# The first attention of a two-layer attention kernel: folding work dealt last, the last pair's inverses and division sooner, and the planned order from four units ahead of the projection

## The chip, the cores and the metric

The kernel runs on one core of a Trainium2 chip. The metric is the device time of one execution in microseconds (us); a measurement is the median of several runs. The core has a matrix engine (TensorE, called PE in the profile), three engines for elementwise work (VectorE or DVE, ScalarE or ACT, GpSimd or POOL), and SyncE (SP), which here only issues DMAs. Each engine works through its own list of instructions in order and waits for the others at semaphores. [...]

## The reference

Two layers work on x (8, 512, 32, 32), batch by batch; T = 1024 positions, 512 channels. Cut to what matters:

```python
# layer 0: eight heads of 64 channels
h = group_norm(xf)
qkv = einsum('oc,bct->bot', qkv_w, h) + qkv_b
q, k, v = (fake_quant(t) for t in split(qkv))     # 8 bits; minimum and maximum over the whole tensor
w = softmax(einsum('bct,bcs->bts', q * scale, k * scale))
a = einsum('bts,bcs->bct', w, v)
x = xf + einsum('oc,bct->bot', proj_w, a) + proj_b
# layer 1: one head of 512 channels
t = tokens(group_norm(x))
q, k, v = t @ wq.T + bq, t @ wk.T + bk, t @ wv.T + bv
out = softmax(q @ k.T / sqrt(512)) @ v
x = x + tokens_back(out @ wp.T + bp)
```

## The kernel before, in words

A first phase (up to about 581 us) norms x, forms q, k and v of all batches, stores them to HBM and collects their extremes, since the quantization needs these over the whole tensor. Then comes a second phase, which the change concerns: attention of layer 0, the projection and layer 1, batch by batch.

**Units.** Layer 0's attention is a generator, `attention()`. Two heads make a pair; a batch has four pairs, written (batch, pair). A unit is one step u: for a pair and one half (512) of the queries, one block s of 128 keys. A pair has 16 units, a batch 64, so units 0 to 63 are batch 0 and unit 64 begins pair (1,0). For each unit TensorE forms the scores `st` (`scores`, line 1007), ScalarE takes their exponential into a tile `pt`, `spare` or `aside`, and the result is split (`split`, line 1038) into an f16 part and the rest in f16, both in `two`: one engine casts, and VectorE subtracts the cast from the exponential (`rest`). In batch 0 the cast is a DMA issued by GpSimd for s = 0, 1 and 4, VectorE's for s = 6, and ScalarE's for s = 2 and 5; blocks s = 3 and 7 stay f32 (`aside`) and are not split. From batch 1, s = 2 and 6 are cast by GpSimd. TensorE then forms the weighted sums of v (`av`) and the sums of the exponentials (`sm`). `scores` runs six to nine units ahead of the weighted sums: a turn of the generator, four units long, begins with the scores of units u+6 and u+7 and ends with the split of u+8 and u+9.

**Work of a pair.** `load_pair` (line 937) fetches q, k and v of the next pair and puts their quantizing on VectorE: two instructions each for q, k and v, and a third for v in batch 0. `finish` (line 1128), after a pair's second half, copies the sums, gathers them into `apart` by two small DMAs, and leaves two pieces of work: `spread`, which adds and inverts them, writes them to HBM and fetches them back broadcast over the partitions; and `divide`, which divides the pair's output `ao`. The projection needs all four.

**Folding.** Layer 1's weights are multiplied with one another ahead of their use (`fold`, line 1734): wq with wk into `wa`, wv with wp into `wm`. The generator yields after each product, 36 steps in all; six of them (`HELD`) are kept for batch 0's layer 1. The others are taken by TensorE, nine ahead of unit 0 and 21 in `scores` (line 1014), one at a time. A fold of two has four products of four steps, then a weighing of the bias and a sum. It also leaves VectorE work: five pieces named "fold", each over `fold_room` or the widened `z`, which the weighing needs, and four named "wa".

**Who orders VectorE.** TensorE's order is that of the text. In the first attention the order of VectorE and ScalarE is that of the text too (`InOrder.strict`); work that is not tied to a unit waits in a list, `dealt`, of entries (unit from which it is due, name, work). At each split, `deal(u)` (line 919) does the first entry of the list that is due, and no more than one; fetching v goes along with the entry ahead of it. `settle(name)` does all of a name at once, where they are needed at the latest: quantized q and k ahead of the first scores of a pair, the divisions ahead of the projection. A cast by DMA is kept in `put_off`, and its subtraction is put in at the split three units later, or where it is needed.

After batch 0's attention and `LEAD` = 2 further turns (units 64 to 71), `InOrder.planned` is set (line 1888): from then on a planner keeps a clock for TensorE, VectorE and ScalarE, adds each operation's cost, and fits side work (`later`, with a time at which it is ready and one at which it is due) into the gaps that it foresees. Then `project(0)` follows, whose half of 16 f32 products is split by one turn of attention, and layer 1 of batch 0 with further turns between.

Of the kernel before, what the change touches and what calls it, by code (L numbers as in the profile page):

```python
# [25 lines left out]
PAIRS = HEADS // 2  # L26
# [20 lines left out]
LEAD = 2  # L47
# [11 lines left out]
def attn_pair_kernel(  # L59
# [97 lines left out]
    def elements(n):  # L157

        return 0.21 + n * 0.957e-3
# [147 lines left out]
    with ExitStack() as fast:  # L307
# [39 lines left out]
        cut, at = {}, 0  # L347
# [44 lines left out]
        with tc.tile_pool(name="p1w", bufs=1) as p1w, tc.tile_pool(  # L392
            name="p1", bufs=2
# [519 lines left out]
        def plain(b, s):  # L913
            return b == 0 and s % 4 == 3
# [2 lines left out]
        dealt = []  # L917

        def deal(u):
            i = next((i for i, (at, *_) in enumerate(dealt) if at <= u), None)  # L920
            if i is not None:
                dealt.pop(i)[2]()
                if dealt[i : i + 1] and dealt[i][2].__name__ == "fetch_v":
                    dealt.pop(i)[2]()
# [12 lines left out]
        def load_pair(b, j, u=None):  # L937

            nm = f"{b}_{j}"
            raws = []  # L940

            def fetch(i, src):
                if (b, j, i) == (0, 0, 2):
                    raw = aop.tile([P, NH, 512], F32, tag="ao", name="raw_first").rearrange(
                        "p h n -> p (h n)"
                    )
                else:
                    raw = raw_p.tile([P, T], F32, tag="raw", name=f"raw_{nm}_{i}")
                nc.sync.dma_start(
                    raw if i < 2 else raw.rearrange("p (t d) -> p t d", t=NT), src  # L950
                )
                raws.append(raw)

            def whole(raw, _, i):
                quant2(raw.rearrange("p (t d) -> p t d", t=NT)[:, 3::4, :], vfs[j], i)

            fetch(0, q_d[b][j])
            fetch(1, k_d[b][j])
            qt = qkp.tile([P, T], BF, tag="q", name=f"q_{nm}")
            kt = qkp.tile([P, T], BF, tag="k", name=f"k_{nm}")  # L960
            vt = qkp.tile([P, NT, P], F16, tag="v", name=f"v_{nm}")
            todo = (qt, kt, vt.rearrange("p t d -> p (t d)"))

            if b == 0:
                vfs[j] = xp.tile([P, 2, 256], F32, tag="x", name=f"vf_{nm}")[:, :, 0:P]

            def quants(i):
                for n, step in enumerate((quant, quant2, *([whole] if i == 2 and b == 0 else []))):
                    name, work = "qk" if i < 2 else "qv", lambda step=step: step(raws[i], todo[i], i)
                    if u is None or InOrder.planned:  # L970
                        dve.later(name, 0.7, work, pe.t + 12.0, 45.0)
                    else:
                        dealt.append((u + (7, 9, 15)[i] + n, name, work))
                        if (i, n) == (0, 1):
                            dealt.append((u + 8, "qk", fetch_v))

            def fetch_v():
                if len(raws) == 2:
                    fetch(2, v_d[b][:, :, bass.ts(j, P)])
                quants(2)  # L980

            if (b, j) == (0, 0):
                fetch(2, v_d[b][:, :, bass.ts(j, P)])
            quants(0)
            quants(1)
            if u is None or InOrder.planned:
                dve.later("qk", 0.0, fetch_v)
            return qt, kt, vt
# [4 lines left out]
        def attention():  # L993
# [13 lines left out]
            def scores(u):  # L1007
                b, j, hf, s = units[u]
                if hf == 0 and s == 0:
                    settle("qk")  # L1010
                nm = f"{b}_{j}_{hf}"
                qt, kt, _ = pairs[b, j]
                st = pair_ps(f"st_{nm}_{s}")
                if (u < 10 or u % 5 == 0) and fold_left[0] > HELD:
                    fold_step()
                awaits(st_free[-2])
                for i, r in enumerate(HALF):
                    mm(
                        st[:, i, :], lhsT=kt[r, bass.ts(s, P)],
                        rhs=qt[r, bass.ts(hf, 512)], start=True, stop=True,  # L1020
                    )
                if u >= 4:
                    need(u - 4)
                if plain(b, s):
                    pt = aside[:, u // 4 % 3].rearrange("p (i k) n -> p i (k n)", i=2)
                elif u < BY_DMA and s in CAST_BY_DMA:
                    at = (u // NT * len(CAST_BY_DMA) + CAST_BY_DMA.index(s)) % 3
                    pt = spare[:, 1 + 2 * at : 3 + 2 * at].rearrange("p i k n -> p i (k n)")
                else:
                    pt = ptp.tile([P, 2, 512], F32, tag="p", name=f"pt_{nm}_{s}")  # L1030
                there = act.do(
                    1.12, lambda: act.activation(pt, st, AF.Exp, scale=esc),
                    max(pe.t + 0.25, ready.get(u - 4, 0.0) + 0.1),
                )
                st_free.append(there)
                pts[u] = pt, there

            def split(u):

                b, j, hf, s = units[u]  # L1040
                pt, there = pts.pop(u)
                if not InOrder.planned:
                    for v in [v for v in put_off if v < u - 2]:
                        put_off.pop(v)()
                    deal(u)
                if plain(b, s):
                    parts[u], ready[u] = pt, there
                    return
                two = partp.tile([P, 2, 2, 512], F16, tag="two", name=f"two_{b}_{j}_{hf}_{s}")
                parts[u] = two  # L1050

                def rest():
                    dve.tensor_tensor(two[:, 1], pt, two[:, 0], ALU.subtract)
                    ready[u] = dve.t

                if u < BY_DMA and s in CAST_BY_DMA:
                    nc.gpsimd.dma_start(two[:, 0], pt)
                    put_off[u] = rest
                    return

                def cast(copy=act.copy):
                    at_hand.add(u)
                    copy(two[:, 0], pt)  # L1063
                    done_at = act.t if copy == act.copy else there + 1.5
                    dve.later("sum", elements(1024), rest, done_at + 0.1, 9.0)

                if b == 0:
                    cast(dve.tensor_copy if s in CAST_BY_DVE else act.copy)
                elif s % 4 == 2:
                    cast(nc.gpsimd.tensor_copy)  # L1070
                elif not InOrder.planned and s == 5:
                    cast(dve.tensor_copy)
                else:
                    act.later("cast", 1.02, cast, there, 7.0)
# [53 lines left out]
            def finish(b, j, hf, u):  # L1128
# [30 lines left out]
                def spread():  # L1159
                    r = rcs[:, n * 16 : (n + 1) * 16]  # L1160
                    dve.tensor_add(r, apart[:, 0, :], apart[:, 1, :])
                    dve.reciprocal(r, r)
                    nc.sync.dma_start(rs_d[n].rearrange("r (p k) -> (r p) k", k=16), r)
                    for i, r in enumerate(HALF):
                        nc.sync.dma_start(
                            rs[r], rs_d[n][2 * i : 2 * i + 2, :].partition_broadcast(CH)
                        )
                    if InOrder.planned:
                        dve.later("ao", elements(1100), divide, dve.t + 7.0, 20.0)
                    else:  # L1170
                        dealt.append((u + 20, "ao", divide))

                if InOrder.planned:
                    dve.later("ao", 0.4, spread, pe.t + 5.0, 8.0)
                else:
                    dealt.append((u + 12, "ao", spread))

            for u in (0, 2, 4):
                for i in (u, u + 1):
# [671 lines left out]
        def advance():  # L1851
            nonlocal done
            done = next(att, B)

        def others():
            steps = None
            for b in range(B):
                if steps is None:
                    yield from project(b)
                    steps = norm1(b)  # L1860
                steps = yield from layer1(b, steps)
# [12 lines left out]
        InOrder.strict = True  # L1874
        while done < 1:
            advance()
        for _ in range(LEAD):
            advance()
        while fold_left[0] > HELD:
            fold_step()  # L1880
# [2 lines left out]
            const.tile([P, 1], F32, name="second_pow"), fourth[:, 0:1], mhalf[:, 0:1], ALU.pow  # L1883
        )
        tc.add_manual_dep(warm.ins, dve.last.name, IN_ORDER, reason="order")
        for e in (dve, act):
            e.t = pe.t
        InOrder.planned = True
        for n in others():
            dense, late = n < 0, n == 2  # L1890
            advance()
# [364 lines left out]
```

## Time and profile before

| | us |
|---|---|
| median of 3 runs (2586.36 to 2592.11) | 2586.4 |
| the profiled execution, its own time | 2591.22 |
| its span in the profile | 2589.4 |
| first scores of unit 0 | 590.68 |
| first scores of units 16, 32, 48, 64 | 617.78, 647.42, 672.24, 696.65 |
| last sums of batch 0's attention end | 705.07 |
| first and second half of the first projection begin | 716.02, 743.15 |

The profile is of one execution, traced by the hardware. Its page gives the busy time of each engine as a share of the span and, in 40 slices of the span (64.7 us each), the busy tenths and the clock that TensorE was granted, in tenths of full speed. A line of the view of waits names the engine and tile that waited, after the arrow the engine and tile it waited for, and then the total in us, the number of times and the longest. A line of the timeline has the start and the length in us, the engine, the line of the kernel (often that of a helper: 91 for VectorE and ScalarE, 209 for TensorE), the operation, the output and inputs with their shapes, the number of instructions merged, and in brackets the idle time just before and what ended it. An f32 product leaves two records on TensorE.

### The profile page before, as it was taken

The numbers are of one execution on the slowest core, as the hardware profiler recorded it, in microseconds if no ns is written. First come the engines' busy times: TensorE is split into PE (matmuls) and PEld (weight loads), VectorE is DVE, ScalarE is ACT, GpSimd is POOL, SyncE is SP. The second block draws the span as 40 slices with busy tenths as digits, with TensorE's granted clock in tenths as the row PEclk, the third lists the DMA queues.
The fourth block names the chain that finished last, engine by engine and source line by source line (L and its number), as shares of the span: only waits on it lengthen the run. The fifth ranks groups of instructions, "written<-read, shape, count | busy, mean of one in ns | idle before, by whom it ended". The sixth has DMA issues, their size and how long they took to land.

```text
span 2589.4 us, 38715 instructions
## 1 busy us (share of the span) xinstructions
PE 2526.8 (98%) x15670; PEld 1751.5 (68%) x15670; DVE 1898.0 (73%) x2748; ACT 1346.6 (52%) x1683; POOL 186.1 (7%) x167
## 2 busy tenths in 40 slices
PE   7999999998989999999999999999999999999998
PEld 4788888872247765775677577657756775777687
DVE  6787777668868777777877788777777777775544
ACT  3222222217947665665566566747665665664121
POOL 0000000001100001000100010010001000100000
PEclk9899999999999999999999999999999999999999
DMA  4333333336622232223222331232232123212211
GB/s 168 129 145 135 117 119 122 130 122 172 152 80 73 67 110 98 62 78 111 86 58 79 116 97 58 95 116 61 78 107 98 46 79 123 83 54 83 86 37 39
DMA packets 160189, 250.69 MB, mean 97 GB/s; under 512 B 27008, under 2 KB 93568, under 8 KB 158464
## 3 DMA queue, kind: packets, MB, share of 16 engines
q1 hardware_dynamic: 125264, 182.81, 21.2%
q10 hardware_dynamic: 30560, 57.71, 6.5%
q0 software_dynamic: 4176, 7.60, 1.7%
q8 instruction: 125, 2.05, 0.3%
q14 instruction: 64, 0.52, 0.1%
HBM read 153.64 MB, written 86.28 MB: 93 GB/s over the span
## 4 chain that ended last, share of the span: by engine, by line
PE 84%; DVE 6%; ACT 3%; issue 1%; DMA 1%; POOL 0%; SPq 0%; ACTq 0%; DVEq 0%; POOLq 0%
PE s L209 15%; PE o L209 13%; PE qkps L209 12%; PE pj L209 9%; PE av L209 7%; PE v2ps L209 7%; PE vps L209 6%; PE g L209 6%; PE st L209 4%; PE sm L209 3%; DVE two L91 2%; ACT pt L91 1%; DVE h L91 1%; PE fold L209 1%; DVE acc L91 1%
## 5 line engine op out<-in xcount | busy, mean ns | idle before, releaser
L91 ACT ACTIVATE pt<-st,esc 128x1024 f32<-128x1024 f32 x467 | 496.6, 1115 | 343.0 <-PE st L209 328.5
L91 DVE TENSOR_TENSOR two<-pt,two 128x1024 f16<-128x1024 f32 x467 | 562.4, 1218 | 145.7 <-POOL two L1063 102.9
L91 ACT CAST two<-pt 128x1024 f16<-128x1024 f32 x345 | 349.9, 1055 | 6.1 <-ACT p L91 5.1
L209 PE MATMUL av<-two,v 128*32 128x512 f16 x3968 | 246.0, 381 | 4.5 <-DVE two L91 3.3
L1063 POOL CAST two<-pt 128x1024 f16<-128x1024 f32 x112 | 146.3, 1306 | 1418.1 <-ACT pt L91 720.4
L209 PE MATMUL s<-g,h 128*128 128x256 f32 x1024 | 233.4, 380 | 0.0
L209 PE MATMUL pj<-ao,wp 128*128 128x512 f32 x512 | 226.3, 600 | 6.2 <-DVE ao L91 6.2
L209 PEld LDWEIGHTS s<-g,h 128*128 128x128 f32 x1024 | 193.0, 190 | 30.9 <-issue 4.3
L91 ACT ACTIVATE u_ring<-qkps,qkbt 128x512 f32<-128x512 f32 x89 | 61.1, 687 | 253.1 <-PE qkps L209 236.2
L209 PEld LDWEIGHTS <-v 128*32 128x32 f16 x3968 | 91.7, 96 | 142.2 <-issue 66.3
L209 PEld LDWEIGHTS pj<-ao,wp 128*128 128x128 f32 x512 | 97.0, 192 | 129.3 <-issue 112.0
L209 PE MATMUL st<-q,k 64*128 64x512 bf16 x1024 | 163.5, 382 | 17.3 <-ACT pt L91 4.9
L209 PE MATMUL s<-g,sums 128*128 128x256 f32 x768 | 178.5, 381 | 0.2 <-DVE p L91 0.2
L209 PE MATMUL o<-p,v 128*128 128x256 f32 x768 | 175.2, 382 | 1.0 <-DVE p L91 1.0
L209 PEld LDWEIGHTS o<-p,v 128*128 128x128 f32 x768 | 144.3, 190 | 27.1 <-issue 5.7
L209 PEld LDWEIGHTS s<-g,sums 128*128 128x128 f32 x768 | 144.6, 190 | 24.5 <-issue 4.6
L209 PE MATMUL sm<-two,ones 128*32 128x512 f16 x1984 | 136.2, 380 | 0.0
L209 PE MATMUL qkps<-half,w_high 128*128 128x512 f32 x480 | 134.5, 403 | 0.0
L209 PE MATMUL qkps<-half,w_low 128*128 128x512 f32 x480 | 132.4, 398 | 1.9 <-DVE half L91 1.9
L209 PEld LDWEIGHTS <-k 64*128 64x128 bf16 x1024 | 34.6, 94 | 146.6 <-issue 139.9
L209 PE MATMUL qkps<-half,w_mix 128*128 128x512 f32 x480 | 132.6, 399 | 0.6 <-DVE half L91 0.6
L209 PE MATMUL v2ps<-wm,h 128*128 128x256 f32 x512 | 119.9, 383 | 1.9 <-ACT g L91 1.3
(225 smaller groups left out, 3909.8 us busy)
## 6 DMA issues: line engine op xcount, KB each, us to landing
rs<-rs_d SPq DMA_DIRECT2D x76, 256.0 KB
x<-in_x_dram SPq DMA_DIRECT2D x32, 512.0 KB
q_d<-wa SPq DMA_DIRECT2D x32, 512.0 KB
k_d<-wa SPq DMA_DIRECT2D x32, 512.0 KB
v_d<-v_ring SPq DMA_DIRECT2D x32, 512.0 KB
raw<-q_d SPq DMA_DIRECT2D x32, 512.0 KB
raw<-k_d SPq DMA_DIRECT2D x32, 512.0 KB
x_d<-h SPq DMA_DIRECT2D x64, 256.0 KB
```

Of the source, the lines that this page charges most:

```text
L91: ins = self.latest = op(*args, **kw).ins
L209: ins = nc.tensor.matmul(ps, lhsT=lhsT, rhs=rhs, **kw).ins
L1063: copy(two[:, 0], pt)
```

## The change

Seven edits, all in the order of work; no product or operation of the computation is added or taken away.

```diff
         def deal(u):
-            i = next((i for i, (at, *_) in enumerate(dealt) if at <= u), None)
-            if i is not None:
+            due = [i for i, (at, *_) in enumerate(dealt) if at <= u]
+            if due:
+                i = next((i for i in due if dealt[i][1] not in ("fold", "wa")), due[0])
                 dealt.pop(i)[2]()
...
-                        dealt.append((u + (7, 9, 15)[i] + n, name, work))
+                        at = u + (7, 9, 15)[i] + n + (8 if b and j else 0)
+                        dealt.append((at, name, work))
                         if (i, n) == (0, 1):
-                            dealt.append((u + 8, "qk", fetch_v))
+                            dealt.append((at, "qk", fetch_v))
...
-                if (u < 10 or u % 5 == 0) and fold_left[0] > HELD:
+                if (u < 4 or u % 4 == 1) and fold_left[0] > HELD:
                     fold_step()
...
                     deal(u)
+                else:
+                    for v in list(put_off):
+                        at_hand.add(v)
+                        dve.later("sum", elements(1024), put_off.pop(v), pe.t, 9.0)
...
-                        dealt.append((u + 20, "ao", divide))
+                        dealt.append((u + (20 if j < PAIRS - 1 else 11), "ao", divide))
...
-                    dealt.append((u + 12, "ao", spread))
+                    dealt.append((u + (12 if j < PAIRS - 1 else 7), "ao", spread))
...
-        for _ in range(LEAD):
+        for _ in range(LEAD - 1):
             advance()
...
-        for e in (dve, act):
-            e.t = pe.t
+        dve.t, act.t = pe.t + 4.5, pe.t + 2.0
         InOrder.planned = True
+        for _, name, work in dealt:
+            dve.later(name, 0.7, work, pe.t + 10.0, 24.0)
+        dealt.clear()
+        advance()
         for n in others():
```

1. `deal` prefers a due entry that is not folding work ("fold" or "wa") and falls back on folding work.
2. The quantizing of a later pair of a later batch, which in the unplanned part is pair (1,1) alone, is due eight units later, and its fetch of v with q's second instruction.
3. The fold steps are taken at units 0 to 3 and then at every fourth unit (5, 9, 13, ... 69) instead of at units 0 to 9 and every fifth (10, 15, ... 60). The weighing of the first fold goes from unit 7 to unit 17.
4. Subtractions still put off when planning begins are given to the planner.
5. For the last pair of a batch in the unplanned part (units 48 to 63), the inverses are due at unit 67 instead of 72 and the division at 71 instead of 80.
6. Planning begins after the turn of unit 64 instead of after that of unit 68. The turn of unit 68 is then planned; the position of the projection in TensorE's order stays.
7. The planner's clocks of VectorE and ScalarE start 4.5 and 2.0 us ahead of TensorE's instead of level with it, and the entries left in `dealt` become side work of the planner.

## The prediction

> **What bounds the kernel now.** I read the page first: who is busy, and in which slices.
>
> ```profile
> PE 2526.8 (98%) x15670; PEld 1751.5 (68%) x15670; DVE 1898.0 (73%) x2748; ACT 1346.6 (52%) x1683; POOL 186.1 (7%) x167
> PE   7999999998989999999999999999999999999998
> PEclk9899999999999999999999999999999999999999
> ```
>
> TensorE is busy 98% of the span, so time can only come from its few waits or from its work, and the change alters no product. Next, the waits of TensorE alone, from 580 to 800 us, where the first attention and the first projection lie.
>
> ```profile
> PE pj L209 <- DVE ao L91: 6.2, 1, 6.2
> PE st L209 <- DVE k L91: 4.6, 1, 4.6
> PE av L209 <- DVE two L91: 3.3, 5, 1.3
> ...
> PE wt_f L209 <- DVE spare L91: 1.4, 1, 1.4
> ...
> PE av L209 <- DVE v L91: 1.1, 1, 1.1
> ```
>
> Two waits stand out, once each: the scores of pair 2 (unit 32) for its keys, and the projection for the last pair's division. From 735 us to the end the same view adds up to 9.8 us, the longest 1.3; so nothing large is to be had later. The timeline of TensorE at the two waits:
>
> ```profile
> 642.17 0.61 PE L209 MATMUL sm<-two,ones 128*32 128x512 f16 x8
> 647.42 0.60 PE L209 MATMUL st<-q,k 64*128 64x512 bf16 x4 [4.64 <-DVE k L91]
> ...
> 648.78 1.93 PE L209 MATMUL av<-aside,vf 128*32 128x512 f32 x8
> ...
> 716.02 2.84 PE L209 MATMUL pj<-ao,wp 128*128 128x512 f32 x6
> 725.06 5.24 PE L209 MATMUL pj<-ao,wp 128*128 128x512 f32 x6 [6.20 <-DVE ao L91]
> ```
>
> After each wait the work is slow for some us: aside's eight products take 1.93 instead of 1.03, six records of the projection 5.24 instead of 2.84. By the starts of the following instructions that costs 1.6 and 2.1 us. VectorE's timeline says what is late:
>
> ```profile
> 627.88 0.69 DVE L91 CUSTOM_DVE_ANT_0 fold_room<-wn_v,gn_row 128x512 f32<-128x512 f32 x1
> ...
> 635.55 0.68 DVE L91 TENSOR_SCALAR spare<-ones,z 128x32 f32<-128x32 f32 x4
> ...
> 646.62 0.75 DVE L91 TENSOR_SCALAR k<-raw,bhi 128x1024 bf16<-128x1024 f32 x1
> ...
> 714.55 1.01 DVE L91 TENSOR_TENSOR rcs<-apart 128x16 f32<-128x16 f32 x1
> ...
> 723.73 1.28 DVE L91 SCALAR_TENSOR_TENSOR ao<-ao,scl,kept_u 128x1024 f32<-128x1024 f32 x1 [1.44 <-DMA kept_u<-rs_d]
> ```
>
> Five pieces of folding work and two loads stood ahead of pair 2's quantizing, so k came at 646.62. The last pair's inverses came at 714.55, though its sums were complete at 705.07 (the end of aside's last sums).
>
> **What the Trainium skill says.** "TensorE: Matmul & The Clock Gate", What's actually happening: an idle window of about 3.4 us halves the clock for about as long. The trace agrees: waits of 4.64 and 6.20 us were followed by slow products, that of 1.43 us (at 600.76) was not. "Trainium Architecture — The Big Picture", Inside one NeuronCore: each engine has its own instruction stream and meets the others only at semaphores; so what stands behind a waiting division waits as well, as here the 7 us of TensorE behind ao. "DMA: Bandwidth & Descriptors", Issuing engines are not separate DMA queues: all DMAs share 16 engines. The trace agrees: the casts by DMA took 6.4 us to land in 600 to 614 us, beside the 2 MB load of x, and 3.4 in 614 to 640.
>
> **The change part by part.** I worked the dealing rule through by hand, unit by unit, for both kernels; the old order reproduces VectorE's timeline.
>
> Folding dealt last. Pair 2's k moves from the deals at units 30 and 31 to 26 and 27, some 6 us sooner (1.5 us a unit). It is 4.6 us late, so that wait goes: 4.6 gained. The slow 1.6 after it I don't count: the pair after the wait took 24.8 us (672.24 less 647.42), the next one 24.4, as ScalarE sets the pace there (24.14 busy of 25 us, 680 to 705). The folding work, four at 0.69 and 0.16 + 0.68, is 3.6 us; it goes to units 36 to 45. There VectorE has, for a pair, 12 subtractions at 1.14, 2 casts at 0.7, 4.4 of quantizing, 1.6 of inverses and division, so 21.1, and with it 24.7 against a pair of 24.4: I charge 0.5.
>
> Fold steps spread out. Units 0 to 15 had 12 steps and get 7; the weighing goes from unit 7 to 17. ScalarE's waits for TensorE there were 0.46, 1.44, 0.26 and 1.88, and a copy of 0.59 moves away: up to 4.4 could go. But the weighted sums of units 4 and 5 need subtractions that VectorE, busy without a gap from 596, ends at 605.2; following ScalarE from there, unit 16 starts at 614.4 instead of 617.78: 3.4 gained. The steps reappear: 12 instead of 9 in units 16 to 61, and two at 65 and 69, each 1.06 to 1.13 us of TensorE. TensorE had 22.79 busy of 25 us (680 to 705), so 2.2 free a pair, and one step more fits; if it didn't, it would cost 1.1 a pair. I charge 0.3 for the three pairs and 1.0 of the 2.2 for the last two, where the gaps were only 0.61 and 0.27.
>
> DMAs and queues. The 2 MB load of x frees with the weighing, so SP issues it near 616 instead of 602.28; it meets the casts by DMA of units 16, 17 and 20, whose subtractions came 5.6 us after issue. With 6.4 of landing that is 0.8 charged. At worst three casts are late by 3: 3 us.
>
> The last pair. The inverses are dealt at unit 68 (was 72), the division at 71 (was 80). Count from T, the end of the last sums (705.07 before). The two gathers are issued at T+1.2; elsewhere an 8 KB gather lands 2.7 after (937.59 to 940.31): T+3.9. VectorE, free at T+2.5, waits 1.4 there, and the inverses end at T+4.3. Write issued T+4.5, broadcast 1.5 later (777.23 to 778.67), landing 4.6 to 6.2 after that (1308.44 to 1313.03; 717.51 to 723.73): T+10.6 to T+12.2. Behind the inverses stand unit 69's cast and subtraction, then 70's and 68's: done near T+8.4 instead of T+7.8. Then VectorE waits for the broadcast, and behind the division (1.2) stands unit 71's subtraction (1.14): T+13.0 to T+14.6. TensorE, which had passed at T+9.5, wants that at about T+10.5: the wait has moved from the projection to the weighted sums, and is 2.5 to 4.1 us. 1.0 us of products later the projection starts, at T+14.0 to T+15.6, and its first half takes 13.75 without a break: T+27.8 to T+29.4, where it ended at T+33.74 (738.81). That is 4.4 to 6.0 gained, less 0 to 2.1 if the clock drops again. I take 4.0; the bounds are 0 (a gather late by 4 us) and 8.3 (6.2 + 2.1, all of it).
>
> Planned order four units sooner. Pair (1,1)'s four quantizings of 0.67 (712.75 to 719.27 before) leave VectorE's way to the projection and become chores beside it. The projection's first half lasts 13.75; VectorE has there 5.7 of evictions and statistics, four subtractions, 4.6, and these 2.7: 13.0, so they fit barely. Without that cover, unit 80's scores would wait 1 to 2 us. The fetch of v for that pair (512 KB, 716.45) leaves SP's way ahead of the broadcast. The v quantizing, which was left in a list until it was forced (the 1.1 us wait above), can now be planned: 1.0 gained. GpSimd's power operation comes ahead of unit 74's cast and waits for unit 71's subtraction, so that cast starts at about T+15; its user comes at T+28, so it is hidden by 10 us. The added chores for units 72 and 73 are work that was there.
>
> Sum: 4.6 - 0.5 + 3.4 - 0.3 - 1.0 - 0.8 + 4.0 + 1.0 = 10.4 us. The profiled execution took 2591.22 (span 2589.4), 4.8 over the median of the runs; the saving is taken from the median: 2586.4 - 10.4 = 2576.0.
>
> **Rivals.**
> 1. The wait for the division is only renamed. If the broadcast lands at T+14 or later, VectorE holds unit 71 until T+16.5 and the tail gains 1 at most; with a late burst of x, 5 to 7 in all: 2580 to 2583. For it: the division stands in an order that can't be left. Against it: where a division waited for its broadcast elsewhere, that had taken 4.6 three times and 5.0 to 5.3 three times (9.7 once, at 2381).
> 2. All of the tail goes: landing by T+9, no clock drop, and ScalarE's pace kept in the pairs: 2586.4 - 15 = 2571. Against it: the chain of T+10.6 above is made of the shortest times seen.
> 3. Slower: the plan from unit 68 on starts from other clocks (VectorE 4.5, ScalarE 2.0 ahead), and orders all that follows. If each of the eight batches got one wait of over 1.3 us, the 10.4 are gone, and at 2.0 each it ends at 2592; its place would be the scores beside the projections. Against it: those waits are 9.8 us in 1850 now, and a plan's clock is set right wherever an engine waits.
> 4. The change does nothing: k of pair 2 still late, the tail as before, 2586. The hand-worked order speaks against it.
>
> **How the numbers follow.** Likeliest case 0.52 (2571.5 to 2580), rival 1 0.22, rival 2 0.12, rival 3 0.10, rival 4 0.04. Predicted 2576. From rival 2's time to past rival 1's is 2570.5 to 2584.5; outside are rivals 3 and 4 and some of rival 2, below 0.2. 0.3% is 7.8 us, about what a measurement of this kernel can tell from no change: faster means below 2578.6. That is rival 2 and some five sixths of the likeliest: 0.55. Slower means above 2594.2, about half of rival 3: 0.06. The rest, 0.39, is between.
>
> **What would show it.** Right: no TensorE wait for k near 640; unit 16's first scores 24 us after unit 0's (was 27.1); the inverses about 4 us after T; the division before unit 71's subtraction; a TensorE wait for `two` of 2.5 to 4 just ahead of the projection, none inside it. Wrong: a pair of units 16 to 63 that takes over 25.5 us; division later than T+14; waits of TensorE after 735 adding up to over 15 us; a new wait of scores for q or k beside the first projection.

## The result, and the profile after

| | before | after |
|---|---|---|
| median, us (11 runs each) | 2588.39 (2586.36 to 2592.11) | 2582.56 (2580.45 to 2586.38) |
| ratio, with 95% interval | | 0.9977 [0.9968, 0.9987] |
| profiled execution, its own time (span) | 2591.22 (2589.4) | 2581.92 (2580.1) |

The kernel is 5.8 us faster, 0.23%; forecast was 10.4 us and 2576.0. The page of the kernel after, its first line:

```profile
PE 2525.0 (98%) x15670; PEld 1751.9 (68%) x15670; DVE 1897.2 (74%) x2747; ACT 1346.8 (52%) x1684; POOL 185.3 (7%) x167
```

Nothing shows at this scale, except that TensorE has the same 15670 records of products: only its waits and its clock can have moved. The waits of TensorE from 580 to 800 us (columns as before: who waited for whom, total, times, longest):

```profile
PE av L209 <- DVE two L91: 5.6, 7, 1.7
PE st L209 <- ACT pt L91: 4.5, 9, 0.8
PE av L209 <- DMA two<-spare: 2.3, 2, 1.8
...
```

The waits for k (4.6), for ao (6.2) and for v (1.1) are gone. A wait that was not there before has come: weighted sums that wait for a DMA, the cast of `spare` into `two`. To see where the time went I cut both traces at the first scores of units 0, 16, 32, 48 and 64, at T (the end of batch 0's last sums) and at the end of the projection's first half. Lengths in us:

```
                 0-16  16-32  32-48  48-64  64-T  T-half   sum
before           27.1   29.6   24.8   24.4   8.4   33.7   148.1
after            24.1   29.6   24.6   24.7   9.5   28.9   141.4
forecast, gain   +3.4   +4.6-0.8  -0.5-0.3    -1.0  +4.0
measured, gain   +3.0    0.0   +0.2   -0.3  -1.1   +4.9    +6.7
```

The stretch 16 to 32 is the surprise: the wait for k, 4.6 us, has gone from its end, and the stretch is as long as before. After the projection's first half the rest of the span is 0.7 us shorter (1850.6 before, 1849.9 after). That makes 7.4 us by the traces; another 1.8 lie ahead of unit 0 (590.68 before, 588.85 after), where the program was not changed, and unit 0 begins anywhere from 586.1 to 590.7 in the traces of this case. VectorE's timeline after, in the stretch 16 to 32:

```profile
624.65 1.22 DVE L91 TENSOR_TENSOR two<-spare,two 128x1024 f16<-128x1024 f32 x1 [3.66 <-DMA two<-spare]
...
626.77 1.23 DVE L91 TENSOR_TENSOR two<-spare,two 128x1024 f16<-128x1024 f32 x1 [0.82 <-DMA two<-spare]
```

And TensorE's:

```profile
624.76 0.40 PE L209 MATMUL av<-two,v 128*32 128x512 f16 x4 [1.83 <-DMA two<-spare]
625.92 0.40 PE L209 MATMUL av<-two,v 128*32 128x512 f16 x4 [0.77 <-DVE two L91]
626.79 0.40 PE L209 MATMUL av<-two,v 128*32 128x512 f16 x4 [0.46 <-DMA two<-spare]
628.05 0.62 PE L209 MATMUL av<-two,v 128*32 128x512 f16 x4 [0.86 <-DVE two L91]
628.43 1.09 PE L209 MATMUL sm<-two,ones 128*32 128x512 f16 x8
```

Two subtractions wait for their casts, 3.66 and 0.82 us, and TensorE behind them waits four times, 3.9 us in all; then the clock drops (eight sums in 1.09 us, which take 0.60 elsewhere). Over the stretch 16 to 32 the granted clock was 0.94, and TensorE was busy 25.1 of 29.6 us. What was issued ahead, first on SP's queue, then by GpSimd:

```profile
614.43 0.94 SPq L1241 DMA_DIRECT2D h<-in_x_dram  x2
617.91 0.34 SPq L950 DMA_DIRECT2D raw<-k_d  x1
```

```profile
615.23 0.53 POOL L1063 DMA_DIRECT2D two<-spare  x1 [5.89 <-ACT spare L91]
616.73 1.01 POOL L1063 DMA_DIRECT2D two<-spare  x1 [0.96 <-ACT spare L91]
```

The weighing, now at unit 17 (613.30 to 614.3 on TensorE), frees the tile of x; SP sends x's two loads (1 MB each) at 614.43, and the casts of units 16 and 17 come 0.8 and 2.3 us behind. They land 9.4 and 10.0 us after their issue, and their subtractions begin then. The tail, on VectorE and then on TensorE:

```profile
705.06 0.17 DVE L91 TENSOR_TENSOR rcs<-apart 128x16 f32<-128x16 f32 x1 [2.15 <-DMA apart<-kept_u]
...
713.08 1.28 DVE L91 SCALAR_TENSOR_TENSOR ao<-ao,scl,kept_u 128x1024 f32<-128x1024 f32 x1 [3.48 <-DMA kept_u<-rs_d]
714.28 1.22 DVE L91 TENSOR_TENSOR two<-pt,two 128x1024 f16<-128x1024 f32 x1
```

```profile
715.55 0.40 PE L209 MATMUL av<-two,v 128*32 128x512 f16 x4 [1.75 <-DVE two L91]
716.31 14.00 PE L209 MATMUL pj<-ao,wp 128*128 128x512 f32 x32
```

With T at 701.38 the inverses begin at T+3.7, the division at T+11.7, and unit 71's subtraction stands behind it; TensorE waits for that subtraction, and then the projection begins at T+14.9 and runs its first 32 records without a break.

### The profile page after: what moved, and what is told of

Read it like the earlier page. It is cut to its first block, busy times and chain, and to the rows that moved or that the text cites. A ratio compares the mean times of both kernels' runs of the same rounds, so it can differ in the third digit from the quotient of the medians.

```text
span 2580.1 us, 38716 instructions
## 1 busy us (share of the span) xinstructions
PE 2525.0 (98%) x15670; PEld 1751.9 (68%) x15670; DVE 1897.2 (74%) x2747; ACT 1346.8 (52%) x1684; POOL 185.3 (7%) x167
## 4 chain that ended last, share of the span: by engine, by line
PE 85%; DVE 5%; issue 2%; ACT 2%; DMA 1%; POOL 0%; SPq 0%; ACTq 0%; DVEq 0%; POOLq 0%
PE s L209 15%; PE o L209 13%; PE qkps L209 12%; PE pj L209 9%; PE av L209 8%; PE v2ps L209 7%; PE vps L209 6%; PE g L209 6%; PE st L209 4%; PE sm L209 3%; DVE two L91 2%; ACT pt L91 1%; DVE h L91 1%; PE fold L209 1%; DMA two<-spare 1%
## 5 line engine op out<-in xcount | busy, mean ns | idle before, releaser
L209 PEld LDWEIGHTS s<-g,h 128*128 128x128 f32 x1024 | 193.1, 190 | 30.8 <-issue 4.3
```

Of the source, the lines that this page charges most:

```text
L209: ins = nc.tensor.matmul(ps, lhsT=lhsT, rhs=rhs, **kw).ins
```

## The experiments

The theory: the k wait goes, as forecast, but x's load, moved by the weighing, makes the casts of units 16 and 17 late and costs the same again. Rivals: the k wait is replaced by VectorE's load or the added fold steps; or the casts are late for another reason (k's fetch, SP's queue). The medians of the kernel before beside these runs were 2590.4 to 2590.5 us (first eight runs; single runs 2588.4 and 2589.5 for the last four), so ratios, not differences to another chip's median, compare them with before. Differences to the change are given by the medians; the kernel before beside the change took 2588.4, so they are uncertain by about 2 us. The quoted text ahead of each result is what was expected before the run.

**Edit 1 alone**, on the kernel before:

```diff
-            i = next((i for i, (at, *_) in enumerate(dealt) if at <= u), None)
-            if i is not None:
+            due = [i for i, (at, *_) in enumerate(dealt) if at <= u]
+            if due:
+                i = next((i for i in due if dealt[i][1] not in ("fold", "wa")), due[0])
```

> The kernel before with the first edit alone (folding work dealt last; fold steps, last pair and planning as before). Stretches of TensorE are named by the first scores of their units; before they were, in us: units 0 to 16 27.1, 16 to 32 29.6, 32 to 48 24.8, 48 to 64 24.4, 64 to the end of the last sums 8.4, from there to the end of the projection's first half 33.7, in all 148.1; after the whole change 24.1, 29.6, 24.6, 24.7, 9.5, 28.9, in all 141.4. Theory: this edit by itself takes the wait for pair 2's keys away, and what the whole change lost in units 16 to 32 comes from the moved fold steps. Then 16 to 32 takes 25 (24.5 to 25.7), the rest is as before, in all 143.6, and the median is 4 to 5 below that of before. Rival: VectorE is simply short of time in units 16 to 32, so the wait for the keys turns into waits for subtractions: 27 to 29 there, and at most 2 off the median.

Measured 2584.33, ratio 0.9977 [0.9967, 0.9988]. Stretches 27.1, 25.0, 24.4, 24.4, 8.4, 33.6: the k wait is gone from TensorE's waits, 16 to 32 is 4.6 shorter, and VectorE's folding work, dealt later, lengthens no other pair. This one edit of the seven is worth by itself what all seven gave.

**Edit 3 alone**, on the kernel before:

```diff
-                if (u < 10 or u % 5 == 0) and fold_left[0] > HELD:
+                if (u < 4 or u % 4 == 1) and fold_left[0] > HELD:
```

> The kernel before with the third edit alone (the fold steps at units 0 to 3 and every fourth, the weighing at unit 17). By the dealing order pair 2's keys are now dealt at unit 28 instead of 31, as the folding work itself comes later, so the wait for them should be gone without the first edit. Theory: the load of x (2 MB) now runs into the casts by DMA of units 16 and 17, and that costs what the keys gave: 24.1, 29 to 30, 24.7, 24.7, 9.5, 33.7, in all 146.2, some 2 below before. Rival: the keys still need the first edit: a wait of TensorE for k of over 2 us, 16 to 32 over 31, in all 148 or more.

Measured 2584.03, ratio 0.9973 [0.9962, 0.9983]; stretches 24.2, 29.9, 24.8, 24.5, 9.5, 32.1. Units 0 to 16 gain 2.9. But the prediction had not seen that the later weighing also moves folding work out of k's way: by the dealing rule k comes at unit 28 instead of 31, and its wait is down to 0.6. Yet 16 to 32 doesn't get shorter, since the casts are late here too (they land in 9.3 and 10.2 us, and TensorE's waits for the DMA `two<-spare` are 2.2). So edits 1 and 3 each remove the k wait, and their gains don't add. By its ratio this kernel gains more than the 2 us expected; its stretches account for 3.1.

**All but edit 3**: the change with the old spacing of the fold steps.

```diff
-                if (u < 4 or u % 4 == 1) and fold_left[0] > HELD:
+                if (u < 10 or u % 5 == 0) and fold_left[0] > HELD:
```

> The whole change without its third edit (fold steps as before: units 0 to 9 and every fifth, the weighing at unit 7, so that x is loaded near 602 again). Theory: the keys are in time by the first edit and x is out of the way: 27.1, 25.0, 24.5, 24.4, 8.4, 28.9, in all 138.3; the median 3 below the whole change. Rival: the stall of the whole change in units 16 to 32 has nothing to do with where the fold steps are; then 16 to 32 keeps 28 to 30, and as the start is 3 slower this is level with the whole change or 2 slower.

Measured 2580.36, ratio 0.9962 [0.9948, 0.9975]; stretches 27.3, 25.0, 24.4, 24.4, 8.4, 31.1. Without edit 3 the change is no slower than with it (2.2 us less by the medians, but the intervals overlap), though its tail was worse in this execution than the 28.9 expected: the 3.0 us that edit 3 gains in units 0 to 16 are lost again, with 4.6 in 16 to 32 and 1.1 after unit 64.

**x in eight pieces**: the change, with x's load taken out of the list of due work and issued by ScalarE, one piece of 256 KB at each of units 22, 26, ... 50.

```diff
-                    dealt.append((28, "load", lambda: load_x2(0, nc.sync.dma_start)))
...
+        X_AT = tuple(range(22, 54, 4))
+        def load_x2_part(i):
+            if i == 0:
+                xts[0] = l1p.tile([P, CC, T], F32, tag="h", name="h2_0")
+            hf, cc = divmod(i, CC)
+            h = bass.ts(hf, 512)
+            act.dma_start(xts[0][:, cc, h], x_v[0, :, cc, h])
...
                     deal(u)
+                    if u in X_AT:
+                        load_x2_part(X_AT.index(u))
```

> The whole change, with the load of x for the first projection cut into eight pieces of 256 KB that ScalarE's queue issues at units 22, 26, ... 50, instead of two of 1 MB that SP issues as soon as the weighing is done (614 us). Theory: the casts by DMA of units 16 and 17, which took 9.4 and 10.0 us to be of use, were held up by x alone; they land in 3.5 to 5 again, and 16 to 32 takes 25: 24.1, 25.0, 24.7, 24.7, 9.5, 28.9, in all 136.9, the median 4 to 5 below the whole change. Rival: the weighing at unit 17, the sum at 21 and the four pieces on wa that VectorE gets at units 20 to 30 make this stretch long; then it stays at 28 to 29.6, whatever x does.

Measured 2576.68, ratio 0.9948 [0.9934, 0.9961], 5.9 us below the change. Stretches 23.0, 24.6, 24.6, 24.7, 9.5, 32.9: 16 to 32 is 5.0 us shorter and like its neighbours, with all the folding work and fold steps in place, which refutes the first rival. The casts of units 16 and 17 land 2.8 and 3.9 us after issue. Of the 5.0 us, 3.0 are idle time and 2.0 the slow clock: TensorE is busy 23.1 of 24.6 us here at a granted clock of 1.00, against 25.1 of 29.6 at 0.94. The pieces differ from the change's load in size, in time and in queue; the queue is tried below, size and time were not tried apart. VectorE's timeline of this kernel at the two subtractions that waited 3.66 and 0.82 has no idle time:

```profile
617.07 1.22 DVE L91 TENSOR_TENSOR two<-spare,two 128x1024 f16<-128x1024 f32 x1
...
618.28 1.22 DVE L91 TENSOR_TENSOR two<-spare,two 128x1024 f16<-128x1024 f32 x1
```

The tail was 4 us longer than in the change, though nothing in it was edited. By its timelines the broadcast of the inverses landed 7.55 us after issue (698.22 to 705.77) instead of 6.1, and TensorE waited for unit 71's subtraction, behind the division, and lost clock after that (the projection's first 32 records take 15.86 us instead of 14.00):

```profile
708.25 0.62 PE L209 MATMUL av<-two,v 128*32 128x512 f16 x4 [4.86 <-DVE two L91]
708.62 1.09 PE L209 MATMUL sm<-two,ones 128*32 128x512 f16 x8
709.65 15.86 PE L209 MATMUL pj<-ao,wp 128*128 128x512 f32 x32
```

**The division one unit later**, and so behind unit 71's subtraction:

```diff
-                        dealt.append((u + (20 if j < PAIRS - 1 else 11), "ao", divide))
+                        dealt.append((u + (20 if j < PAIRS - 1 else 12), "ao", divide))
```

> The whole change, with the last pair's division due one unit later (72 instead of 71), so that on VectorE it stands behind unit 71's subtraction instead of ahead of it. The last stretch (from the end of the last sums, T, to the end of the projection's first half) was 28.9 in the whole change, where TensorE waited 1.75 us for that subtraction and worked slowly for a while. Theory: VectorE does the subtraction while the broadcast is on its way; TensorE begins the projection near T+12, and needs the division only 2.6 later, when it is done (T+13): 26 to 27, and 2 to 3 off the median of the whole change; all other stretches as there. Rival: the division only comes 1.2 later for it, and TensorE waits at the projection's fourth product, as in the kernel before: 28 to 29, no gain.

Measured 2576.92, ratio 0.9954 [0.9940, 0.9968], 5.6 us below the change; stretches 23.0, 29.2, 24.6, 24.7, 9.5, 25.4. VectorE's timeline here, and TensorE's first projection:

```profile
707.88 1.22 DVE L91 TENSOR_TENSOR two<-pt,two 128x1024 f16<-128x1024 f32 x1
711.55 1.28 DVE L91 SCALAR_TENSOR_TENSOR ao<-ao,scl,kept_u 128x1024 f32<-128x1024 f32 x1 [2.45 <-DMA kept_u<-rs_d]
```

```profile
711.16 14.06 PE L209 MATMUL pj<-ao,wp 128*128 128x512 f32 x32
```

The division is no earlier (T+11.8), but TensorE no longer waits for a subtraction that waits for the broadcast, and the projection begins at T+11.4 instead of T+14.9. The projection even begins 0.39 us before the division, since its first products use the other pairs.

**Both**, the pieces and the later division (the two diffs above together):

> The whole change with x in eight pieces and the division one unit later. With x in pieces alone the last stretch took 32.9, as the broadcast came back 7.6 us after its issue and TensorE waited 4.9 for unit 71's subtraction, and then worked at half speed. Theory: these are one cause, the division ahead of the subtraction, and a late landing now costs little: 23, 24.6, 24.6, 24.7, 9.5, 27, in all 133.4, and the median 5 to 6 below x in pieces alone. Rival: the lateness is that of the broadcast itself, and shows as a wait for ao inside the projection: 30 to 32.9 in the last stretch, 0 to 2 off.

Measured 2572.26 (2572.18 to 2572.69), ratio 0.9936 [0.9923, 0.9950]: 10.3 us below the change by the medians, and the best of the kernels run. Stretches 24.2, 24.6, 24.6, 24.7, 9.5, 26.2. The waits of TensorE from 580 to 800 us:

```profile
PE st L209 <- ACT pt L91: 5.6, 10, 0.8
PE av L209 <- DVE two L91: 2.0, 3, 1.5
...
```

What is left is mostly ScalarE's pace in the scores, the longest wait 1.5.

**Six fold steps at the start** instead of four, on the kernel with both, to take back the steps at units 65 and 69:

```diff
-                if (u < 4 or u % 4 == 1) and fold_left[0] > HELD:
+                if (u < 6 or u % 4 == 1) and fold_left[0] > HELD:
```

> As the kernel with both (x in pieces, division one unit later), but with fold steps at units 0 to 5, then every fourth from 9 to 65: one step goes from unit 69 to unit 4. In the whole change TensorE worked at half clock from 597 to 601 us, after three gaps of 0.6 in a row for exponentials, where the weighted sums of units 0 and 1 took 1.90 instead of 1.05. Theory: the gaps were left by the steps moved away, so one more step there costs nothing and keeps the clock, and the step less at unit 69 gives 0.5 to 1.0 back: 22.5 to 23.0 in units 0 to 16, 8.8 from 64 to T, the median 0.5 to 1.5 below the kernel with both. Rival: the step delays unit 5's scores and ScalarE, which sets the pace: 24 in units 0 to 16, level or 0.5 slower.

Measured 2573.88 (2571.20 to 2576.32), ratio 0.9941 [0.9927, 0.9954]; stretches 23.0, 26.0, 25.2, 24.4, 8.8, 27.2. The 0.7 us after unit 64 come as expected, and 2.0 are lost in units 16 to 48: no gain over the kernel with both is shown. In 16 to 32 the clock was halved for a while here (0.93 granted), and with both it was not (1.00).

**Edits 1 and 5 without the rest**: the last pair's inverses and division sooner, but planning after two turns as before.

```diff
-                        dealt.append((u + 20, "ao", divide))
+                        dealt.append((u + (20 if j < PAIRS - 1 else 11), "ao", divide))
...
-                    dealt.append((u + 12, "ao", spread))
+                    dealt.append((u + (12 if j < PAIRS - 1 else 7), "ao", spread))
```

> The kernel before with the first and the fifth edit (folding work last; the last pair's inverses and division sooner), but planning from the turn of unit 72 on as before, and pair (1,1)'s quantizing unplanned. With the first edit alone the last stretch took 33.6, with all but the third edit 31.1. Theory: the two halves of the tail's edits need each other: the division now comes at T+13, but behind it VectorE has unit 71's subtraction, four quantizings and seven casts and subtractions in a fixed order ahead of the projection's first eviction, some 11 us; TensorE then waits for evictions (h) inside the projection, 2 to 3 us: 31.5 to 33.5 in all, at most 2 off the first edit alone. Rival: the sooner division is all that counts, and 31 or less is reached without planning.

Measured 2584.11, ratio 0.9978 [0.9971, 0.9985], as edit 1 alone; stretches 27.1, 24.9, 24.4, 24.4, 8.4, 34.6. The sooner division by itself gains nothing; the tail is even longer than the 33.5 expected at most. TensorE has two waits in the tail:

```profile
710.78 0.40 PE L209 MATMUL av<-two,v 128*32 128x512 f16 x4 [1.94 <-DVE two L91]
...
721.76 8.81 PE L209 MATMUL pj<-ao,wp 128*128 128x512 f32 x16 [3.08 <-DVE h L91]
```

In VectorE's fixed order, four quantizings of pair (1,1) and eight subtractions and casts stand between the division and the projection's first eviction (VectorE adding a finished product to x, tile `h`), which comes at 720.97, 9.4 us after the projection's start. The projection waits for an eviction, 3.08 us, and is slow after it. In the change the first eviction comes 3.7 us after the projection's start (716.31 to 720.05), ahead of the quantizings. So the sooner division needs the edits that take the quantizings out of its way. Edits 2, 4, 6 and 7 were not tried apart: edit 2, which puts these quantizings off, may do a part of what the earlier planning does.

The last four tell what makes the casts late: they move x's load or k's fetch, in the kernel before with edit 1 or in the change. Each was timed once, with its profile.

**x's load just ahead of unit 16's exponential**, on ScalarE's queue, on the kernel before with edit 1 (where x was sent at 602):

```diff
                     deal(u)
+                    if u == 15:
+                        load_x2(0, act.dma_start)
...
-                    dealt.append((28, "load", lambda: load_x2(0, nc.sync.dma_start)))
```

> The kernel before with the first edit alone, and nothing else of the change, but the two 1 MB loads of x for the first projection, which SP had issued at about 602, are issued by ScalarE's queue just ahead of unit 16's exponential, that is where the whole change had them. Fold steps, weighing and wa's work are where the kernel before has them. With the first edit alone units 16 to 32 took 25.0, with the whole change 29.6. Theory: the load of x at this place is enough by itself: the casts by DMA of units 16 and 17 are of use only 9 to 10 us after their issue, and 16 to 32 takes 29 to 30. Rival: the collision needs the fetch of q or k that fell into the same moment in the whole change, or the work displaced there; then 25 to 27.

Measured 2585.18; stretches 27.1, 24.9, 24.2, 24.4, 8.4, 34.4. The expectation failed: no loss. The load went out at 612.45 and 612.88, and the casts at 615.96 and 616.97, so 3.5 us behind x and not 0.8; the casts landed in 6.4 and 6.6 us, and only one subtraction waited, 0.76.

**The same, one exponential later**, so that the distance is that of the change:

```diff
+                if u == 17:
+                    load_x2(0, act.dma_start)
                 there = act.do(
...
-                    dealt.append((28, "load", lambda: load_x2(0, nc.sync.dma_start)))
```

> As the last one (first edit alone, x moved to ScalarE's queue), but the two loads of x stand one exponential later, just ahead of unit 17's, so that they are issued about 1 us ahead of the cast by DMA of unit 16, as in the whole change (0.8), and not 3.5 ahead. There units 16 to 32 took 24.9: x was half through when the casts were issued, and the fetch of pair 2's k came only at 620.5. Theory 1 (x alone, at this moment): the casts land after 8 us or more, 16 to 32 takes 28 to 30. Theory 2 (x with the 512 KB of k right behind it, 2.5 us after the first cast in the whole change): the casts land in 5 to 6.5, 25 to 26.

Measured 2588.25; stretches 27.2, 28.6, 24.2, 24.4, 8.4, 33.6. Now x went out at 616.77 and 617.20 and the casts at 618.50 and 619.51, 1.7 us behind. They landed in 7.8 and 10.0 us, and 16 to 32 is 3.7 us longer than in the run before this one, as the first theory has it. The two kernels differ in the time of one load alone. Their subtractions of units 16 and 17 on VectorE, first x early, then x late:

```profile
622.39 2.46 DVE L91 TENSOR_TENSOR two<-spare,two 128x1024 f16<-128x1024 f32 x2 [0.76 <-DMA two<-spare]
```

```profile
626.34 1.23 DVE L91 TENSOR_TENSOR two<-spare,two 128x1024 f16<-128x1024 f32 x1 [2.04 <-DMA two<-spare]
...
629.57 1.23 DVE L91 TENSOR_TENSOR two<-spare,two 128x1024 f16<-128x1024 f32 x1 [2.00 <-DMA two<-spare]
```

**The change with x's load on ScalarE's queue** at the same place (the diff of the run before, on the change; k's fetch stays on SP's):

> The whole change, with the two 1 MB loads of x issued by ScalarE's queue just ahead of unit 17's exponential, so at about the moment where SP issued them in the whole change, while the fetch of pair 2's k stays on SP. Both theories expect what the whole change had, 28.5 to 30 for units 16 to 32, as neither gives a part to the queue that carries x. A third: it is SP's queue that is slow, x and k standing behind one another on it; then the casts land in 5 to 6 and 16 to 32 takes 25 to 26.

Measured 2582.36; stretches 23.0, 30.0, 24.6, 24.7, 9.5, 30.8. x went out at 613.19; the casts landed in 9.7 and 10.4 us and the first subtraction waited 4.02. The queue that carries x plays no part, and the third theory is refuted.

**The change with k's fetch later**, at unit 22 on ScalarE's queue, out of the casts' way:

```diff
-        dealt = []
+        dealt, late_k = [], []
...
-            fetch(1, k_d[b][j])
+            if (b, j) == (0, 2):
+                late_k.append(lambda: fetch(1, k_d[b][j], act.dma_start))
+            else:
+                fetch(1, k_d[b][j])
...
+                    if u == 22:
+                        late_k.pop()()
                     deal(u)
```

> The whole change, with the fetch of pair 2's k (512 KB) moved from SP's queue, where it is issued at 617.9, to ScalarE's, just ahead of unit 22's exponential, some 5 us later. x stays as in the whole change (two of 1 MB, SP, 614.4). Theory 1 (x alone): 16 to 32 stays at 28 to 30. Theory 2 (x and k together): the casts land some 1.5 to 3 us sooner and 16 to 32 takes 25 to 27; k itself is needed only about 10 us later.

Measured 2581.76; stretches 24.2, 28.5, 24.6, 24.7, 9.5, 31.8. With x alone in the way (612.10, casts at 612.91 and 614.40) they landed in 9.1 and 9.3 us. The stretch is 1.1 us shorter than in the change, but not by less waiting: TensorE is idle 5.0 us of it, in the change 4.5, and its clock was 1.00 instead of 0.94. So the first theory holds, and k's part in the loss is not shown to be more than a few tenths of a us.

Read together, the traces tell when a cast behind x's two loads lands. For the first cast behind them, in us:

| kernel | issued, after x's issue | landed, after its own issue | landed, after x's issue |
|---|---|---|---|
| before (600 to 614 us) | 4.5 | 5.3 | 9.8 |
| edit 1, x early | 3.5 | 6.4 | 9.9 |
| edit 1, x late | 1.7 | 7.8 | 9.5 |
| the change | 0.8 | 9.4 | 10.2 |
| the change, x on ScalarE's queue | 0.8 | 9.7 | 10.5 |
| the change, k later | 0.8 | 9.1 | 9.9 |

The last column hardly changes: whenever in these 4.5 us the cast is issued, it lands about 10 us after x. In the change no packet of the casts' queue moves from 615.3 to 620.0, while x's queue moves 1.20 MB.

## Why the prediction was right or wrong

**Folding dealt last: mechanism and size right, gain not kept.** "4.6 us late, so that wait goes": 4.6 by the run of edit 1 alone (29.6 to 25.0). Not charging the slow clock after the wait was right too. The 0.5 charged for VectorE was not needed: 32 to 48 became 0.4 shorter there and 0.2 shorter in the change. What I missed is the overlap: edit 3 by itself takes the folding work away from k, so two of the edits remove one wait. The sum is not touched by that, as it counts the wait once.

**x's load: the step that failed.** "With 6.4 of landing that is 0.8 charged. At worst three casts are late by 3." The place was right (units 16 and 17), the size was not: 4.6 us by the change without edit 3, 5.0 by the pieces of x. The 6.4 came from 600 to 614 us of the kernel before, where x had been sent at 602.28 and the next two casts at 606.74 and 608.12, 4.5 and 5.8 us behind it; they landed in 5.3 and 7.5. In the change the casts were issued 0.8 and 2.3 us behind 2 MB, with 512 KB of k 1 us after, and took 9.4 and 10.0. The working from the landing to the charge was sound: where the casts landed in 6.4 and 6.6 us (edit 1, x early), a subtraction waited 0.76. What was wrong is that the landing was counted from the cast's issue. Counted from x's issue, the same casts of the kernel before give 9.8 us for the first, and 10.2 was measured. The charge also put the slow clock behind the new waits at nothing; it is 2.0 of the 5.0 us. The worst case, three casts late by 3, was too small as well. With 5.0 in place of 0.8 the forecast's sum is 6.2, and 5.8 was measured; that they are so near is in part luck, since other terms are off too, by up to 3 us (below). The test that the prediction named, a pair of over 25.5 us, is what showed it.

"DMA: Bandwidth & Descriptors", Issuing engines are not separate DMA queues, in the Trainium skill says that transfers of all issuing engines share the same 16 engines and interleave. The run with x on ScalarE's queue agrees that the queue doesn't matter (9.7 us of landing against 9.4). But nothing of the casts moved in the 4.7 us from 615.3 to 620.0, so they did not interleave with x from the start. I had cited that section, but took from it only that there is a delay, and its size from a moment that was not the same.

**Fold steps spread: right, with some luck in the size.** 3.4 forecast, 3.0 measured, but 4.1 in four other executions (three with the same fold steps, and the one with six at the start). The difference of 1.1, which the forecast didn't have, is clock: after three gaps of 0.6 us TensorE ran at half speed for 3.4 us in this execution. The timeline of the kernel after:

```profile
595.45 0.39 PE L209 MATMUL st<-q,k 64*128 64x512 bf16 x2 [0.64 <-ACT aside L91]
596.46 0.39 PE L209 MATMUL st<-q,k 64*128 64x512 bf16 x2 [0.61 <-ACT spare L91]
597.46 0.61 PE L209 MATMUL st<-q,k 64*128 64x512 bf16 x2 [0.61 <-ACT pt L91]
598.00 1.90 PE L209 MATMUL av<-two,v 128*32 128x512 f16 x16
599.68 1.07 PE L209 MATMUL sm<-two,ones 128*32 128x512 f16 x8
```

Sixteen such products take 1.05 at the full clock (and eight sums 0.60), at 709.75 and 710.62 of the run with the later division for one. The returned steps: 0.3 charged and 0.3 lost in 48 to 64; 1.0 charged and 1.1 lost at units 65 and 69.

**The last pair: the chain right, the gain above what most executions gave.** The inverses were forecast to end at T+4.3 and ended at T+4.1; broadcast T+10.6 to T+12.2, measured T+11.7; projection T+14.0 to T+15.6, measured T+14.9; gain 4.0 forecast, 4.9 measured here. The wait moved to unit 71's subtraction as said (1.75 us, where 2.5 to 4.1 was forecast), and putting the division behind that takes it away. But with the same tail the stretch was 31.1, 32.9, 30.8 and 31.8 us in other executions, a gain of 0.8 to 2.9 (the old tail took 32.1 to 34.4). The one with a landing at T+13.2 is rival 1's tail. In all nine kernels with the sooner inverses the broadcast took 6.1 to 7.6 us to land, the upper end of the 4.6 to 6.2 in the forecast or more. So the trace of the change shows a good case; its 9.3 us of span against the 5.8 of the medians hold 1.8 of unit 0's earlier start, and the rest may come from this tail.

**Planned order sooner: right.** No wait for v (1.0 forecast; the rest of the span is 0.7 shorter), none for q or k beside the projection. Rival 3 is refuted: TensorE's waits of 735 us to the end are 8.7 us, 9.8 before. The earlier planning and the edits that go with it paid in a way that I had only half seen: the division sooner gains nothing without them. What they give by themselves no run shows.

**Rivals.** Rival 1's total (2580 to 2583) holds the measured time, but not by its mechanism: the tail gave what was forecast, and the loss was in 16 to 32. Rivals 2 and 4 did not occur. The range held the time; the likeliest case, 2571.5 to 2580, did not.

## What to carry to other kernels

When an edit moves a load, price the collision by when the load is issued, and not by a landing time that a small transfer had at another moment: here a cast of 256 KB behind 2 MB landed about 10 us after the load's issue. That cost 0.76 us of one engine's time, and no TensorE time, where the casts were issued 3.5 us behind the load and their users came late enough, and 3.7 to 5.0 us of the stretch where they were issued 0.8 to 2.7 behind it. Move such a load to where no small transfer is needed soon, or cut it into pieces there as well; which of the two did it here was not tried apart. And in an engine's fixed order put an operation that waits for a round trip behind the ready work that another engine needs: one place in VectorE's order was worth 5.6 us by the medians here, and 4.4 with x in pieces.

## What the runs showed of the hardware that I had not expected

A cast by DMA issued 0.8 to 2.5 us behind two loads of 1 MB does not get its share early: in the five kernels that have it so it landed after 9.0 to 10.4 us, about 10 us (9.8 to 10.5) after the load for the first cast; with x in pieces and later it took 2.8 to 3.9. What keeps the casts' packets back (for 4.9 us in the change) was not tried.

TensorE dropped to half clock after three gaps of 0.6 us within 2.6 us, but not always: with the same fold steps and gaps, units 0 to 16 took 24.1 or 24.2 us in four executions and 23.0 in three. "TensorE: Matmul & The Clock Gate", What's actually happening, in the Trainium skill has the clock fall after an idle window of about 3.4 us and calls the window free-running, so that the moment varies between runs. The window agrees, and the traces show what decides: the stretches of half clock that they record between 580 and 800 us are 3.41, 6.83 or 10.24 us long. If the time is cut into windows of 3.41 us at these borders, the three gaps lay in one window wherever the clock dropped (in the change, but for the last 0.13 us, 593.92 to 597.33, TensorE busy 1.68 of 3.41 us, half clock from 597.33 to 600.75), and were divided between two where it did not (in the run with the later division 592.92 to 596.33 and 596.33 to 599.75, busy 2.20 and 2.61). So the window was idle for only about half its length, and no gap was longer than 0.64 us: it need not be idle throughout. Where the limit lies was not worked out.

The write of the inverses and their broadcast back took 7.5 us from the issue of the write (705.55 to 713.08 in the change), and the broadcast alone 6.1 to 7.6 between executions; what makes it late in some of them stays open.
